# Runs of counts, early projections and 29 dense chunks in a graph layer with a mixture of experts

## The chip, the core and the metric

The kernel runs on one core of one Trainium2 chip. Its engines each work through a queue of their own: TensorE (PE, with PEld for its weight loads), VectorE (DVE), ScalarE (ACT), GpSimd (POOL), and SyncE (SP), which mostly starts DMAs. The metric is the device time of one launch in microseconds (us), the median over several runs.

## The reference

6250 nodes have 256 features each, and 200,000 edges lead from `src` to `dst`, sorted by `dst`. A graph convolution and a residual projection feed a top-2 mixture of 64 experts, then `y` is normalised over the nodes, added to the features, and layer-normed.

```python
deg_out = jnp.clip(jax.ops.segment_sum(ones, src, num_segments=n), 1.0)
deg_in = jnp.clip(jax.ops.segment_sum(ones, dst, num_segments=n), 1.0)
h = feats * jax.lax.rsqrt(deg_out)[:, None]
m = jax.ops.segment_sum(h[src], dst, num_segments=n) * jax.lax.rsqrt(deg_in)[:, None]
gc = m @ W_gc + b_gc
x = gc + (feats @ W_res + b_res)
core = _moe_ff(x, Wg, bg, w1, b1, w2, b2)
y = x + core
```

## The kernel before

**Stages.** The nodes lie in 50 tiles of 125 (`TP`, `NT`), two of which make a pair. The edges lie in groups of 128.

*Degrees.* In 28 turns (`for i in range(NGR // CG)`) DVE builds two tables of matches, `hot_row` and `hot_col`, and PE multiplies them into `degp`, 56 matmuls a turn (L523). Turns 1 to 25 each hold a projection of one pair by `W_res` as well (`residual`, matmuls at L290 in `projected`), whose result ACT copies out of one of the two banks "pr" (L467) and SP writes to `r_dram`. At i = 2 DVE has a long piece of work (`split` of the remaining edges and what follows), and ACT has twelve activations (L507) that wait for its end. Behind the last turn DVE turns `degp` into `degs`, two projections by `W_gc` run (`firsts_p`), `pd` (L557) folds the degrees by tile, and `s_out` is the factor of each node; a chain on DVE then ends in `key`.

*Opening.* For each pair, `halves` takes the projection by `W_gc`, scales it by `s_out` into rows of two parts (ACT the rounded part, L651; DVE the remainder, L653), and SP writes them to `h_dram`. `steps_of` then multiplies the rows by `back` (L666), which leaves each node's difference to its neighbour, and keeps them in SBUF for the dense chunks (`pair_of`, by ACT L669 and DVE L670). Counts of the first chunk run between.

*Dense chunks.* The edges to the low nodes are dense. `_plan` cuts them into chunks (`DENSE`), each with `n` parts of `k` groups, with windows of `w` columns. For each group one matmul, the count (L740), multiplies `lo` (where the source lies in its tile, made by DVE at L709, eight groups at a time) by `hotk` (the window's match, DVE L269, eight at a time). The `k` groups of a part add up in one PSUM bank (pool `ps_c`, five banks). At the end of each part ACT copies the bank into `words` (`put_in`, L723), and DVE adds the part's first column one part later (`carried`, L775). `apart` unpacks `words` into `counts`, and 50 multiplies (L784) of a chunk form the sums of its nodes. The counts for the next chunk but one are put ahead of the multiplies of the running one, part by part at even distances.

*Gather.* The edges to the high nodes are thin: POOL fetches 128 rows of `h_dram` at a time (L615, a ring of eight), and two matmuls add them up (L620, L621), window by window. A window's sums are copied out by ACT (L1071).

*x_step.* While the chunks run, finished pairs of nodes go through the bias, the transposition (L868), the logits (L877) and the top-2, at fixed multiplies of a chunk.

**Order.** The order on each engine is the order of the program text (`tc.manual_schedule()`). `dense()` yields pieces of work with a cost, and a loop behind it puts a gather in whenever the costs added up reach the next multiple of `every`, which spreads the gathers evenly over that sum; behind a window's last gather it holds the next for `HOLD` = 1.5.

What follows the chunks (the rest of the routing, the experts, the normalisations) is not touched by the change.

Of the kernel before, what the change touches and what calls it, by code (L numbers as in the profile page):

```python
# [66 lines left out]
OPENING, SECOND = 48, 80  # L67
# [93 lines left out]
def gnn_moe_kernel(ctx, tc, x_in, x_turned, src, dst, bases, nexts, firsts, parts, lasts, runs, W_gc, b_gc, W_res, b_res, Wg, bg, w1, b1, w2, b2,  # L161
# [76 lines left out]
    with tc.tile_pool(name="edges", bufs=1) as ep, \  # L238
# [37 lines left out]
        pair_of = {p: ep.tile([TP, 2, 2 * D], F32R, name=f"h{p}", tag=f"h{p}") for p in range(KEPT)}  # L276
# [22 lines left out]
        with tc.tile_pool(name="late", bufs=1) as lp, tc.tile_pool(name="both", bufs=2) as bp, \  # L299
# [164 lines left out]
            def residual(t0):  # L464
# [4 lines left out]

            dstf = lp.tile([128, NGR], F32, name="dstf", tag="dst")  # L470
# [14 lines left out]
                    neg[:, ND + c:ND + c + 1]) for c, (g0, k) in enumerate(GATHER)]  # L485
            for i in range(NGR // CG):
# [32 lines left out]
                if i == 10:  # L519
                    placed()  # L520
                for c in range(CG):
                    r = c % 2
                    T.matmul(degp[64 * r:64 * r + NT], hot_col[:, c // 2, :, r],  # L523
                             bytes_of[:, c // 2, :, r, :], start=(c0 + c < 2), stop=(c0 + c >= NGR - 2))
# [30 lines left out]
            firsts_p = [projected(0, banks[1], w_gc), projected(2, spare_bank, w_gc)]  # L555
# [38 lines left out]
        with tc.tile_pool(name="xs", bufs=1) as xs, tc.tile_pool(name="hotg", bufs=2) as hg, \  # L594
# [5 lines left out]
            for i, a, b, clear in ((0, 0, 9, V), (0, 9, NU, G), (1, 0, NU, G)):  # L600
                clear.memset(words[i][:, a:b, :], 0)
# [6 lines left out]
            for i in range(NR):  # L608
# [3 lines left out]
                ring.append(r)  # L612

# [27 lines left out]
            HB = 4  # L641
            after = xs.tile([TP, 2, D + 2], F32, name="z")[:, 0, :TP]
            G.tensor_scalar(after, iota_f[:TP, :TP], -1.0, pidx[:TP], op0=ALU.add, op1=ALU.is_equal)
            back = hg.tile([128, HB, WIN], F32R, name="hot")[:TP, 0, :TP]
            G.tensor_tensor(back, ident[:TP, :TP], after, ALU.subtract)
# [12 lines left out]
            def steps_of(p):  # L658
# [8 lines left out]
                if p >= KEPT:  # L667
                    pair_of[p] = ep.tile([TP, 2, 2 * D], F32R, name=f"h{p}", tag=f"h{p}")
# [28 lines left out]
            lo_bufs = [hc.tile([128, PAIRS // 2, 128, 2], U16, name=f"lo{i}", bufs=1) for i in range(3)]  # L697
            for lo in lo_bufs:
                G.memset(lo[:, :, TP:, :], 0)
                G.memset(lo[:, :, TP:TP + 1, :], UNIT_CODE)  # L700
# [31 lines left out]
            def count(g):  # L732

                c, j, i = groups[g]
                g0, k, w, n = DENSE[c]
                if i == 0:
# [3 lines left out]
                T.matmul(pc, los[g // PAIRS][:, r // 2, :, r % 2, 0], hots[g // PAIRS][:, r // 2, :NU * w, r % 2],  # L740
                         start=(i == 0), stop=(i == k - 1))
                if i == k - 1:
# [4 lines left out]
                    carried(1)  # L747
                    at, pc = live["at"][j % 8], pc.rearrange("p (u w) -> p u w", w=w)
                    if j == 0:
                        live["adds"], live["carry"], live["puts"] = [], [], []  # L750
                    if c == 0 and j == 0:
                        live["puts"].append(put_in(words[0][:, :, :w], pc).ins)
                    else:
                        if j == 0:
                            step = nc.values_load(step_i[0:1, c:c + 1], engines=(DVE_E,), min_val=0, max_val=WIN - 1,
                                                  skip_runtime_bounds_check_because="clipped to the window")
                            put = put_in(words[c % 2][:, :, 1:w], pc[:, :, 1:])
                            to, had = words[c % 2][:, :, 0:1], words[(c - 1) % 2][:, :, ds(step, 1)]
                        else:
                            put = put_in(words[c % 2][:, :, 1:][:, :, ds(at, w - 1)], pc[:, :, 1:])  # L760
                            to = had = words[c % 2][:, :, ds(at, 1)]
                        for a in live["adds"]:
                            tc.declare_no_dep(put.ins, a, reason="other columns of the window")
                        live["carry"].append((to, pc[:, :, 0:1], had, j))
                        live["puts"].append(put.ins)
                if r in making:
                    making[r](g // PAIRS + 2)
                if i == k - 1 and j == n - 1:
                    carried(0)

            def carried(but):

                while len(live["carry"]) > but:
                    to, more, had, j = live["carry"].pop(0)
                    add = V.scalar_tensor_tensor(to, more, 1.0 / UNIT, had, op0=ALU.mult, op1=ALU.add).ins  # L775
                    tc.add_manual_dep(add, live["puts"][j].name, SYNCED, reason="its bank, and the column of the part in front")
                    for a in live["puts"][j + 1:]:
                        tc.declare_no_dep(add, a, reason="columns behind it")
                    live["adds"].append(add)
# [163 lines left out]
            def x_step(c, t):  # L943
# [7 lines left out]
                    ((0, 2, 4, 6), 9, 19, (22, 24, 26, 27), (28, 29, 32, 36, 39))  # L951
# [30 lines left out]
            def dense():  # L982
# [24 lines left out]
                for c in range(1, ND):  # L1007
                    g0, k, w, n = DENSE[c]
                    us = max(0.03 + 0.0071 * w, (n * (0.19 + k * (0.105 + 0.0089 * w)) / 0.85 - 9.0) / (n * k))
                    for j in range(n):  # L1010
                        at = 1 + j * 34 // n if c == 1 else NT * (c - 2) + 35 + j * NT // n
                        todo.setdefault(at, []).extend((us, g) for g in range(g0 + j * k, g0 + j * k + k))
                for c in range(ND):
                    for t in range(NT):
                        for us, g in todo.get(NT * c + t, []):
                            yield us, lambda g=g: count(g)
# [941 lines left out]
```

## Time and profile before

| | us |
|---|---|
| median of 3 runs | 1522.32 |
| lowest and highest run | 1515.85, 1525.04 |
| the profiled execution | 1522.74 |
| its span, first to last instruction | 1521.0 |
| PE busy | 1371.6 (90%) |
| DVE busy | 901.8 (59%) |
| POOL busy | 770.0 (51%) |
| ACT busy | 674.3 (44%) |

In the profile's rows a time stands first, then the engine, the line of the kernel, the operation, what it writes and reads, its shape and how many such instructions follow one another (x56). Brackets show how long the engine was idle before it and what ended that. A matmul's duration is a modelled one and contains the filling of a pipeline, so where matmuls follow one another the distance from start to start says what each takes. In a list of waits, a row names who waited for whom, the us in all, how often, and the longest.

### The profile page before, as it was taken

Reading aid. Unit: us, or ns where it says so; the run is one execution under the profiler, and the core shown is the slowest. Engines: PE = TensorE matmul, PEld = TensorE weight load, DVE = VectorE, ACT = ScalarE, POOL = GpSimd, SP = SyncE. Lnnn points to the kernel's source line nnn. Section 1 sums busy time; section 2 is a strip of 40 time slices with the busy share of each in tenths; the row PEclk is TensorE's granted clock in tenths of the full one; section 3 lists DMA queues with packets and bytes.
Section 4 is the critical chain, followed back from the end, with each engine's and each line's share of the span. In section 5 each row is a group of like instructions: output and inputs, shape, how many; then the busy total and the mean of one; then the engine's idle time right before and its main releaser. Section 6 shows DMA issues by size and latency. Waiting matters only on the chain. (4 is left out here: it accounts for less than half of the span.)

```text
span 1521.0 us, 29996 instructions
## 1 busy us (share of the span) xinstructions
PE 1371.6 (90%) x8943; PEld 1054.2 (69%) x8943; DVE 901.8 (59%) x2514; ACT 674.3 (44%) x1938; POOL 770.0 (51%) x871
## 2 busy tenths in 40 slices
PE   3997988898999999999999984899999999997995
PEld 3786866566767666666666764788798887886652
DVE  9997776575776766666666647523233332221887
ACT  1232554345565666665566632322222233332257
POOL 6201037777776676665566611266566666663000
PEclk8998999899999999999999995899999999999997
DMA  9463748787888889887888737888699898785925
GB/s 282 133 174 101 218 139 219 201 245 232 242 248 239 232 228 250 227 237 206 222 221 242 214 101 160 211 250 270 191 287 280 259 300 248 238 267 165 266 76 149
DMA packets 214161, 329.79 MB, mean 217 GB/s; under 512 B 36844, under 2 KB 149008, under 8 KB 213988
## 3 DMA queue, kind: packets, MB, share of 16 engines
q1 hardware_dynamic: 159392, 173.57, 42.0%
q0 software_dynamic: 47696, 147.12, 32.3%
q10 hardware_dynamic: 6900, 7.07, 1.6%
q8 instruction: 74, 1.21, 0.3%
q14 instruction: 99, 0.81, 0.2%
HBM read 266.53 MB, written 73.68 MB: 224 GB/s over the span
## 5 line engine op out<-in xcount | busy, mean ns | idle before, releaser
L615 POOL DMA_INDIRECT r<-h_dram,srcg x441 | 459.2, 1041 | 286.1 <-PE pc L740 160.4
L784 PE MATMUL sm<-h,counts 125*128 125x512 f32 x1500 | 530.5, 441 | 0.0
L723 ACT ACTIVATE words<-pc 128x119 f32 (+7 forms) x682 | 191.2, 280 | 249.5 <-PE pc L740 230.1
L784 PEld LDWEIGHTS sm<-h,counts 125*128 125x128 f32 x1500 | 258.2, 197 | 10.3 <-issue 1.9
L1656 ACT ACTIVATE hT<-ph,b1c 128x128 f32<-128x128 f32 (+3 forms) x256 | 108.2, 423 | 295.1 <-PE ph L1654 272.8
L775 DVE SCALAR_TENSOR_TENSOR words<-pc,words 128x17 f32 x681 | 125.7, 185 | 139.0 <-ACT words L723 114.7
L1654 PE MATMUL ph<-xgT,w1s 128*128 128x128 f32 (+8 forms) x1024 | 206.6, 348 | 0.9 <-issue 0.9
L740 PE MATMUL pc<-hotk,lo 128*128 128x136 bf16 (+6 forms) x1122 | 198.7, 233 | 4.7 <-DVE words L775 2.7
L729 ACT ACTIVATE counts<-words 125x1152 fp32r<-125x1152 uint8 (+1 forms) x180 | 197.4, 1098 | 0.3 <-DVE words L775 0.3
L1691 PE MATMUL py<-w2s,hT 128*128 128x256 f32 (+1 forms) x800 | 192.7, 384 | 0.0
L1654 PEld LDWEIGHTS ph<-xgT,w1s 128*128 128x128 f32 x1024 | 170.7, 192 | 29.0 <-issue 9.9
L1615 POOL DMA_INDIRECT y_dram<-ys,dest x124 | 119.1, 961 | 114.6 <-DVE ys L1669 59.8
L740 PEld LDWEIGHTS <-lo 128*128 128x128 fp8e5 x1122 | 86.4, 101 | 128.2 <-issue 105.3
L1615 POOL DMA_INDIRECT xg<-x_dram,ids x124 | 120.3, 970 | 86.9 <-DVE ids L1295 47.8
L620 PE MATMUL pg<-r,hot 128*128 128x258 f32 x441 | 139.0, 315 | 22.0 <-DMA r<-h_dram,srcg 20.6
L1691 PEld LDWEIGHTS py<-w2s,hT 128*128 128x128 f32 (+1 forms) x800 | 144.4, 188 | 20.5 <-issue 0.3
L1669 DVE TENSOR_TENSOR ys<-py,b2s 128x256 f32<-128x256 f32 (+3 forms) x124 | 52.4, 423 | 165.8 <-PE py L1691 136.6
L621 PE MATMUL pg<-r,hot 128*128 128x256 f32 x441 | 125.1, 284 | 0.0
L1639 DVE COPY xgT<-pte 128x256 f32<-128x256 f32 (+8 forms) x64 | 38.5, 601 | 131.7 <-PE pte L1637 131.7
L709 DVE TENSOR_TENSOR lo<-place_in,floor_in 128x1000 uint16<-128x1000 uint16 x141 | 95.4, 676 | 30.7 <-PE pc L740 25.3
L620 PEld LDWEIGHTS pg<-r,hot 128*128 128x128 f32 x441 | 85.7, 194 | 37.3 <-DMA r<-h_dram,srcg 22.5
L269 DVE TENSOR_TENSOR hotk<-key,iota 128x1088 bf16<-128x1088 bf16 (+6 forms) x141 | 98.4, 698 | 4.1 <-issue 4.1
(403 smaller groups left out, 1845.7 us busy)
## 6 DMA issues: line engine op xcount, KB each, us to landing
w1s<-in_L_gnn_w_dram SPq DMA_DIRECT2D x64, 512.0 KB
w2s<-in_L_gnn_w_dram SPq DMA_DIRECT2D x64, 512.0 KB
y_dram<-h_dram SPq DMA_DIRECT2D x97, 128.0 KB
yr<-y_dram SPq DMA_DIRECT2D x25, 448.0 KB
b2s<-in_L_gnn_b_dram SPq DMA_DIRECT2D x64, 128.0 KB
r<-h_dram,srcg POOLq DMA_INDIRECT x441
z_dram<-zeros ACTq DMA_DIRECT2D x7, 903.0 KB
x<-in_x_turned_dram SPq DMA_DIRECT2D x12, 500.0 KB
```

What stands on the lines that cost most here:

```text
L615: G.indirect_dma_start(out=f32(r[:, :2 * D]), out_offset=None, in_=h_dram[:, :], in_offset=bass.IndirectOffsetOnAxis(ap=idx, axis=0))
L620: T.matmul(pg, hot, r[:, D:], start=first, stop=False)
L621: T.matmul(pg[:, :D], hot, r[:, :D], start=False, stop=last)
L723: return S.activation(to, pc, AF.Copy, scale=1.0 / UNIT)
L729: S.activation(counts[:, t0:t1, :], each[:TP, u:u + t1 - t0, :WIN, b], AF.Copy, accum_out=read_sums[:, 6 * c + i:6 * c + i + 1])
L740: T.matmul(pc, los[g // PAIRS][:, r // 2, :, r % 2, 0], hots[g // PAIRS][:, r // 2, :NU * w, r % 2], start=(i == 0), stop=(i == k - 1))
L775: add = V.scalar_tensor_tensor(to, more, 1.0 / UNIT, had, op0=ALU.mult, op1=ALU.add).ins
L784: T.matmul(sm, counts[:, t, :], hrow(t), start=(t == 0), stop=(t == NT - 1))
L1615: w = G.indirect_dma_start(**kw)
L1654: T.matmul(ph[:, :m], w1s[:, kk, c * 128:(c + 1) * 128], xgT[:, kk, :m], start=(kk == 0), stop=(kk == 1))
L1656: S.activation(hT[:, c, :m - apart], ph[:, :m - apart], AF.Gelu, bias=b1_e[:, c:c + 1])
L1691: T.matmul(py[:n], hT[:, c, k * 128:k * 128 + n], w2s[:, c, :], start=(c == 0), stop=(c == 3))
```

## The change

- *Runs of eight.* The counts of a chunk are put ahead of a multiply in runs that begin at each eighth group (`PAIRS`, the groups that one `lo` and one `hotk` serve) or at a chunk's first, not part by part. Up to three parts lie side by side in a bank (`most_of`). ACT copies a bank's parts when the last is counted (`copied_in`), and DVE adds their first columns one bank later.
- *Pacing.* The counts and the x_step have no cost of their own in the pacing sum; each multiply carries `step_us(c)`, taken from the chunks whose counts run then.
- *Plan.* `SECOND` is 112 in place of 80. The plan then has 29 dense chunks in place of 30, 1116 dense groups in place of 1122, and 447 gathered groups in 28 windows in place of 441 in 27.
- *Early projections.* `firsts_p` goes. Twelve pairs (`EARLY_P`) are projected by `W_gc` while the degrees are counted: one ahead of turn 0, three after turn 0's counts, seven ahead of turn 2's, one after turn 26's. ACT copies them into `early_p`. `w_gc` is loaded right behind the first part of x, ahead of `w_res`. The kept pairs take other buffers (`new_pair`).
- *The odd ones of the twelve* are scaled by POOL (two instructions a pair), ACT only copies them, and POOL takes the remainder in place of DVE (two more a pair).
- *Clearing in order of use.* POOL clears the ends of `lo` first, makes `back`, scales the first odd pair, clears its part of `words[0]`, scales the other odd pairs, sets the ring, and then clears `words[1]`.
- *x_step.* The turn comes at the 11th step in place of the 9th, the logits at the 20th in place of the 19th, the top-2 from the 23rd in place of the 22nd.

```diff
-OPENING, SECOND = 48, 80
+OPENING, SECOND = 48, 112
...
+        EARLY_P = KEPT
+        early_p = [ep.tile([TP, 2, 2, D], F32, name=f"p{j}", tag=f"h{j}") for j in range(EARLY_P // 2)]
...
             x_quad(0)
+            nc.sync.dma_start(out=w_gc, in_=W_gc.rearrange("(k p) d -> p k d", p=128))
+            x_quad(1)
             nc.sync.dma_start(out=w_res, in_=W_res.rearrange("(k p) d -> p k d", p=128))
-            for q in range(1, QUADS):
+            for q in range(2, QUADS):
                 x_quad(q)
-            nc.sync.dma_start(out=w_gc, in_=W_gc.rearrange("(k p) d -> p k d", p=128))
...
+            def ahead_of_degrees(p):
+                pr = projected(2 * p, ps_a.tile([128, 512], F32, name="pr"), w_gc)
+                S.copy(early_p[p // 2][:, p % 2], pr)
+
+            jobs = {-1: range(0, 1), 0: range(1, 4), 2: range(4, EARLY_P - 1), NGR // CG - 2: range(EARLY_P - 1, EARLY_P)}
...
+            for p in jobs[-1]:
+                ahead_of_degrees(p)
             for i in range(NGR // CG):
...
+                if i == 2:
+                    for p in jobs[2]:
+                        ahead_of_degrees(p)
                 for c in range(CG):
...
                 if 0 < i <= NT // 2:
                     residual(2 * i - 2)
+                if i != 2:
+                    for p in jobs.get(i, ()):
+                        ahead_of_degrees(p)
...
-            firsts_p = [projected(0, banks[1], w_gc), projected(2, spare_bank, w_gc)]
...
-            for i, a, b, clear in ((0, 0, 9, V), (0, 9, NU, G), (1, 0, NU, G)):
-                clear.memset(words[i][:, a:b, :], 0)
+            lo_bufs = [hc.tile([128, PAIRS // 2, 128, 2], U16, name=f"lo{i}", bufs=1) for i in range(3)]
+            for lo in lo_bufs:
+                G.memset(lo[:, :, TP:, :], 0)
+                G.memset(lo[:, :, TP:TP + 1, :], UNIT_CODE)
+            after = xs.tile([TP, 2, D + 2], F32, name="z")[:, 0, :TP]
+            G.tensor_scalar(after, iota_f[:TP, :TP], -1.0, pidx[:TP], op0=ALU.add, op1=ALU.is_equal)
+            HB = 4
+            back = hg.tile([128, HB, WIN], F32R, name="hot")[:TP, 0, :TP]
+            G.tensor_tensor(back, ident[:TP, :TP], after, ALU.subtract)
+            for p in range(1, EARLY_P, 2):
+                for u in range(2):
+                    one = early_p[p // 2][:, 1, u, :]
+                    G.tensor_scalar(one, one, s_out[:, 2 * p + u:2 * p + u + 1], None, op0=ALU.mult)
+                if p == 1:
+                    for clear, a, b in ((V, 0, 9), (G, 9, NU)):
+                        clear.memset(words[0][:, a:b, :], 0)
...
+            G.memset(words[1], 0)
...
             def halves(t):
-                ps = firsts_p[t // 2] if t < 4 else projected(t - 1, (banks[1], spare_bank)[t // 2 % 2], w_gc)
+                p = t // 2
+                ps = early_p[p // 2][:, p % 2] if p < EARLY_P else projected(t - 1, (banks[1], spare_bank)[p % 2], w_gc)
+                scaled = p < EARLY_P and p % 2
                 rows = held_rows[t // 2] = [stages[(u - NT) % len(stages)] for u in (t - 1, t)]
                 for u in range(2):
-                    S.activation(rows[u][:, :D], ps[:, u, :], AF.Copy, scale=s_out[:, t - 1 + u:t + u])
+                    if scaled:
+                        S.copy(rows[u][:, :D], ps[:, u, :])
+                    else:
+                        S.activation(rows[u][:, :D], ps[:, u, :], AF.Copy, scale=s_out[:, t - 1 + u:t + u])
                 for u in range(2):
-                    V.scalar_tensor_tensor(rows[u][:, D:], ps[:, u, :], s_out[:, t - 1 + u:t + u], f32(rows[u][:, :D]),
-                                           op0=ALU.mult, op1=ALU.subtract)
+                    if scaled:
+                        G.tensor_tensor(rows[u][:, D:], ps[:, u, :], f32(rows[u][:, :D]), ALU.subtract)
+                    else:
+                        V.scalar_tensor_tensor(rows[u][:, D:], ps[:, u, :], s_out[:, t - 1 + u:t + u],
+                                               f32(rows[u][:, :D]), op0=ALU.mult, op1=ALU.subtract)
...
                 if i == 0:
-                    live["pc"] = ps_c.tile([128, 512], F32, name="pc")
-                r = g % PAIRS
-                pc = live["pc"][:, :NU * w]
+                    if j == 0:
+                        carried(0)
+                        live["adds"], live["puts"], live["ended"] = [], [], []
+                    most = most_of(c)
+                    if j % most == 0:
+                        live["bank"] = ps_c.tile([128, 512], F32, name="pc")
+                    live["pc"] = live["bank"][:, j % most * NU * w:(j % most + 1) * NU * w]
...
+                    if j % most_of(c) == most_of(c) - 1 or j == n - 1:
+                        copied_in(c)
...
+            def most_of(c):
+                return min(3, 512 // (NU * DENSE[c][2]))
+
+            def copied_in(c):
+                w, bank = DENSE[c][2], []
+                carried(1)
+                for j, at, pc in live["ended"]:
...
-                    ((0, 2, 4, 6), 9, 19, (22, 24, 26, 27), (28, 29, 32, 36, 39))
+                    ((0, 2, 4, 6), 11, 20, (23, 25, 26, 27), (28, 29, 32, 36, 39))
...
-                        todo.setdefault(at, []).extend((us, g) for g in range(g0 + j * k, g0 + j * k + k))
+                        for g in range(g0 + j * k, g0 + j * k + k):
+                            if g % PAIRS == 0 or g == g0:
+                                run = todo.setdefault(at, [])
+                            run.append(g)
+
+                def spent(c):
+                    if c >= ND:
+                        return 13.0, 5.0
+                    g0, k, w, n = DENSE[c]
+                    return 13.9 + n * k * (0.02 + 0.0071 * w), 5.0 + n * (0.19 + k * (0.105 + 0.0089 * w))
+
+                def step_us(c):
+                    te, ve = (0.7 * a + 0.3 * b for a, b in zip(spent(c + 1), spent(c + 2)))
+                    return max(te / 0.83, ve / 0.78) / NT
...
-                        yield 0.22, lambda c=c, t=t: multiply(c, t)
+                        yield step_us(c), lambda c=c, t=t: multiply(c, t)
                         if 4 <= t < 44:
-                            yield 0.04, lambda c=c, t=t: x_step(c, t)
+                            yield 0.0, lambda c=c, t=t: x_step(c, t)
```

More of the change, by code (lines that the diff above doesn't have):

```diff
@@ L275, in gnn_moe_kernel, with new_pair @@
         KEPT = NT // 2 - QUADS
-        pair_of = {p: ep.tile([TP, 2, 2 * D], F32R, name=f"h{p}", tag=f"h{p}") for p in range(KEPT)}
+        EARLY_P = KEPT
+        early_p = [ep.tile([TP, 2, 2, D], F32, name=f"p{j}", tag=f"h{j}") for j in range(EARLY_P // 2)]
+        pair_of = {}
+        def new_pair(p):
+            to = p + EARLY_P // 2 if p < KEPT - EARLY_P // 2 else p - KEPT + EARLY_P // 2 if p < KEPT else p
+            pair_of[p] = ep.tile([TP, 2, 2 * D], F32R, name=f"h{p}", tag=f"h{to}")
+        for p in range(KEPT - EARLY_P // 2):
+            new_pair(p)
         quad_of = [ep.tile([128, 4, 2, TP], F32, name=f"x{q}", tag=f"h{KEPT + q}", padded_shape=[128, 4, 2, 128])
@@ L666, in steps_of @@
                         T.matmul(bank[:, u, :], back, rows[u][:, k * D:(k + 1) * D], start=(k == 0), stop=(k == 1))
-                if p >= KEPT:
-                    pair_of[p] = ep.tile([TP, 2, 2 * D], F32R, name=f"h{p}", tag=f"h{p}")
+                if p not in pair_of:
+                    new_pair(p)
                 S.copy(pair_of[p][:, :, :D], bank)
@@ L746, in count @@
                             skip_runtime_bounds_check_because="clipped to what the window leaves")
[L747 to L750, printed above, removed]
+                    live["ended"].append((j, live["at"][j % 8], live["pc"].rearrange("p (u w) -> p u w", w=w)))
+                    if j % most_of(c) == most_of(c) - 1 or j == n - 1:
+                        copied_in(c)
@@ L751, in count @@
+                if r in making:
+                    making[r](g // PAIRS + 2)
+                if i == k - 1 and j == n - 1 and c in (0, ND - 1):
+                    carried(0)
+            def most_of(c):
[4 more added lines that the diff above has]
+                for j, at, pc in live["ended"]:
                     if c == 0 and j == 0:
                         live["puts"].append(put_in(words[0][:, :, :w], pc).ins)
-                    else:
[L754 to L769, printed above, removed]
+                        continue
+                    if j == 0:
+                        step = nc.values_load(step_i[0:1, c:c + 1], engines=(DVE_E,), min_val=0, max_val=WIN - 1,
+                                              skip_runtime_bounds_check_because="clipped to the window")
+                        put = put_in(words[c % 2][:, :, 1:w], pc[:, :, 1:])
+                        to, had = words[c % 2][:, :, 0:1], words[(c - 1) % 2][:, :, ds(step, 1)]
+                    else:
+                        put = put_in(words[c % 2][:, :, 1:][:, :, ds(at, w - 1)], pc[:, :, 1:])
+                        to = had = words[c % 2][:, :, ds(at, 1)]
@@ L771, in carried @@
+                    for a in live["adds"]:
+                        tc.declare_no_dep(put.ins, a, reason="other columns of the window, another bank")
+                    bank.append((to, pc[:, :, 0:1], had))
+                    live["puts"].append(put.ins)
+                live["carry"].append((bank, len(live["puts"])))
+                live["ended"] = []
             def carried(but):
                 while len(live["carry"]) > but:
-                    to, more, had, j = live["carry"].pop(0)
@@ L775, in carried @@
[L775 to L779, printed above, removed]
+                    bank, upto = live["carry"].pop(0)
+                    for to, more, had in bank:
+                        add = V.scalar_tensor_tensor(to, more, 1.0 / UNIT, had, op0=ALU.mult, op1=ALU.add).ins
+                        tc.add_manual_dep(add, live["puts"][upto - 1].name, SYNCED,
+                                          reason="its bank, and the column of the part in front")
+                        for a in live["puts"][upto:]:
+                            tc.declare_no_dep(add, a, reason="columns behind it, another bank")
+                        live["adds"].append(add)
```

17 lines of the change are left out of this document (4 added, 13 removed).

## The prediction

> **What bounds the kernel now.** I read the page's engine table first, then the busy time by stage, then the chain. The chain that ended last covers only the final pass over the output, so the stages themselves say what the change is worth. They are the degrees (0 to 127.5 us), the opening in which h is written (to 198.5), the first four dense chunks (to 324), the other 26 (to 909), and the experts and the output, which the change does not touch.
>
> ```profile
> span 1521.0 us, 29996 instructions
> 0.00:127.50 127.50, 101.46 (x1770) 84.75 (x1771) 120.92 (x103) 29.65 (x87) 32.56 (x108) 0.93 0.68 191
> 127.50:198.50 71.00, 61.62 (x344) 53.87 (x344) 50.14 (x120) 33.25 (x79) 5.11 (x27) 0.93 0.55 168
> 198.50:324.00 125.50, 105.73 (x706) 75.80 (x706) 80.88 (x220) 54.26 (x157) 86.21 (x79) 0.90 0.72 196
> 324.00:909.00 585.00, 553.94 (x3215) 397.99 (x3213) 385.64 (x1396) 348.09 (x1063) 372.97 (x362) 0.99 0.81 224
> ```
>
> The columns are PE, PEld, DVE, ACT and POOL busy, the granted clock, the DMA share and GB/s. In the last row PE is busy for 554 of 585 us and no other engine for more than 386. So PE sets this stage, and what PE has to do there is what counts. Its time is read from start to start in the timeline of PE.
>
> ```profile
> 256.73 0.42 PE L740 MATMUL pc<-hotk,lo 128*128 128x136 bf16 x4
> 256.96 0.48 PE L784 MATMUL sm<-h,counts 125*128 125x512 f32 x1
> ...
> 503.92 0.39 PE L784 MATMUL sm<-h,counts 125*128 125x512 f32 x1
> 504.16 0.22 PE L740 MATMUL pc<-hotk,lo 128*128 128x102 bf16 x1
> 504.20 0.47 PE L784 MATMUL sm<-h,counts 125*128 125x512 f32 x1
> 504.51 0.22 PE L740 MATMUL pc<-hotk,lo 128*128 128x102 bf16 x1
> ```
>
> A multiply that follows an fp32 matmul takes 0.24 us (503.92 to 504.16). One that follows a count takes 0.31 (504.20 to 504.51), and the count itself 0.04. So every place where a run of counts ends costs 0.04 + 0.08 = 0.12 us, and a count with another behind it costs 0.075 (four counts of 136 columns take 0.23).
>
> **The change part by part.** *Runs of counts, 29 chunks, 447 gathers.* I counted through dense() and the pacing loop by their source, for the old plan and the new. For the old one this gives 742 counts and 366 gathers from the fifth chunk on and 75 gathers before it, which the rows confirm up to one count.
>
> ```profile
> 324.00:909.00 585.00, 154.52 (x743) 63.25 (x741) 0.99 0.81 224
> ...
> 198.50:324.00 125.50, 26.36 (x75) 14.90 (x75) 0.90 0.72 196
> 324.00:909.00 585.00, 112.63 (x366) 70.83 (x366) 0.99 0.81 224
> ```
>
> From the fifth chunk on there are 1300 multiplies, 611 ends of runs and 131 counts with another behind them. After the change there are 1250, 106 and 594, with 366 gathers as before. That is -50 x 0.234 = -11.7, -505 x 0.12 = -60.6 and +463 x 0.075 = +34.7: **-37.6 us**. At these prices (0.24 a gather, 0.65 a window of gathers) the old stage comes to 489 us of its 585. The other 96 us are the x_step work (23 pairs in both versions), waits and halved clock. One chunk of 26 less takes some 3.5 us of that, which makes **-41**.
>
> In the first four chunks the runs save little, because 3 to 11 groups a part are runs already, and the chunks grow: the prices give 98.8 us before and 100.8 after, with 81 gathers for 75. POOL is the tight one here, with fetches end to end:
>
> ```profile
> 244.40 0.95 POOL L615 DMA_INDIRECT r<-h_dram,srcg  x1 [0.30 <-issue]
> 245.65 0.94 POOL L615 DMA_INDIRECT r<-h_dram,srcg  x1 [0.30 <-issue]
> ```
>
> Six more at 1.25 us are +7.5 and PE's own sum is +2.0. I take **+5**, near POOL's end.
>
> The waits of that stage are the unknown. The rows below are for 206 to 910 us.
>
> ```profile
> POOL r L615 <- PE pc L740: 160.4, 173, 69.1
> DVE words L775 <- ACT words L723: 114.7, 160, 4.4
> PE pg L620 <- DMA r<-h_dram,srcg: 20.6, 14, 3.9
> PE sm L868 <- DVE xr L858: 14.3, 17, 1.8
> L723 ACT ACTIVATE words<-pc 128x119 f32 (+7 forms) x682 | 191.2, 280 | 249.5 <-PE pc L740 230.1 <-PE pg L621 3.7 <-PE sm L784 2.7
> ```
>
> The waits of ACT and DVE cost nothing while PE runs. PE's 14.3 us on xr should shrink, since the turn comes two multiplies later and DVE no longer waits for ACT after every part. Against that, eight copies in a row hold ACT for 8 x 0.28 = 2.24 us, and the copy of a finished gather window stands behind them, with PE's next gather behind that copy. Bounds: -10 (the xr waits mostly gone), +12 (28 windows at 0.4). I take 0. Banks are no new wait: a run of eight fills 2.7 of five, and DVE empties them a run later. The new pacing and the later x_step turns add no instruction and are priced in these counts and waits.
>
> *Twelve projections during the degrees.* These rows show PE and ACT in that stage.
>
> ```profile
> 19.28 2.10 PE L523 MATMUL degp<-hot_row,hot_col 128*50 128x128 fp8e4 x56 [2.17 <-DVE hot_col L492]
> 21.31 3.26 PE L290 MATMUL pr<-w_res,x 128*125 128x256 f32 x8
> 30.97 2.16 ACT L507 ACTIVATE wide<-kd 128x44 f16<-128x44 bf16 x12 [13.24 <-DVE first L418]
> 33.03 0.56 ACT L467 COPY rx<-pr 125x512 f32<-125x512 f32 x1
> 36.11 3.19 PE L523 MATMUL degp<-hot_row,hot_col 128*50 128x128 fp8e4 x56 [11.53 <-DVE hot_col L492]
> 42.00 1.75 PE L523 MATMUL degp<-hot_row,hot_col 128*50 128x128 fp8e4 x56
> ...
> 121.42 1.99 PE L290 MATMUL pr<-w_res,x 128*125 128x256 f32 x8
> 123.34 1.75 PE L523 MATMUL degp<-hot_row,hot_col 128*50 128x128 fp8e4 x56
> 125.70 1.75 PE L523 MATMUL degp<-hot_row,hot_col 128*50 128x128 fp8e4 x56 [0.60 <-DVE hot_col L492]
> ```
>
> A projection takes 1.92 us of PE (121.42 to 123.34), so twelve take 23. PE's holes here are 2.17, 11.53 and 0.60 us, with perhaps 2 before the first count: 17 us, and a delay of 6 us at least. It will be more. Seven projections are put ahead of the counts of i = 2, for the hole of 11.53. But "pr" has two banks, so the third needs ACT's copy of the first, and this copy stands on ACT behind the twelve L507, which wait for DVE until 30.97. The rows show it: the residual that began at 21.31 was copied only at 33.03. So two projections run by 28, PE then stands until 33.13 + 0.58 = 33.7, and five follow: 9.6 us, and 1.5 more because PE comes out of a pause slowly (the counts at 36.11 took 3.19 us, those at 42.00 1.75). That is 44.8. The counts and the residual of i = 2 (3.6) and the counts and residual of i = 3 (3.6) put the counts of i = 4 at 52.0 instead of 42.0. From there both run at PE's 3.6 us a turn, the late one without some 2 us of mask waits that the old one has in 42.00 to 123.34 (22 turns, 81.3 us). The twelfth projection adds 1.92 before the last counts, where PE waited 0.60 anyway. Sum: the last counts start at 42 + 10 + 22 x 3.6 + 1.7 + 1.9 = 134.8 instead of 125.7, **+9**; bounds +6 and +11.
>
> What is gained behind it: the two old projections no longer stand in front of pd.
>
> ```profile
> 128.94 0.22 DVE L554 TENSOR_TENSOR degs<-dsb,rise 128x63 f32<-128x63 f32 x1
> 130.94 0.32 PE L557 MATMUL pd<-fold,degs 128*125 128x50 f32 x2
> ```
>
> degs is ready at 129.2, so pd moves by **-1.7**, and s_out with the key chain behind it.
>
> *The opening.* POOL is let go at 136.2 (call it T), and pairs leave PE every 2.36 us.
>
> ```profile
> 136.21 2.89 POOL L601 MEMSET words<- 128x1056 int32 x2 [25.03 <-issue]
> 145.31 1.42 PE L666 MATMUL pc<-r,hot 125*125 125x256 f32 x4
> 150.71 0.83 PE L666 MATMUL pc<-r,hot 125*125 125x256 f32 x4
> 153.07 0.82 PE L666 MATMUL pc<-r,hot 125*125 125x256 f32 x4
> L643 POOL TENSOR_SCALAR z<-iota_f,pidx 125x125 f32<-125x125 f32 x1 | 0.7, 738 | 0.0
> L1745 POOL TENSOR_TENSOR fb<-fb,bet 125x512 f32<-125x512 f32 x1 | 1.3, 1276 | 0.0
> ```
>
> The second pair's steps ran at T + 9.1. Now that pair's low half is POOL's, and in POOL's order it stands behind everything that is cleared and behind all twelve scalings: small clears and "back" 2, scalings 12 x c, clearing 0.9 + 0.6 + 2.0, then two subtractions of 0.7 (half of the 512-wide row). For c the row with two operations on 125 columns gives 0.74, twice that for the width is 1.5; with one operation instead of two I take 0.8. Sum 16.5: the second pair comes at T + 16.8, **+7.7**. Clearing in order of use thus hides nothing here, as the scalings are the longer part. Pairs 3 to 12 then have no projection. An odd one takes ACT 0.4, POOL 1.4, PE 0.7 and ACT 0.6 in a chain that the even one fits beside: 3.4 us for two instead of 4.7, **-6.7** over ten pairs, and 1.5 for PE's slow start: **+2.5**. With c at 0.5 it is -1, with 1.5 it is +11. The remaining pairs go on at 2.36.
>
> Sum: 9 - 1.7 + 2.5 + 5 - 41 = -26. Against this execution (1522.74 us around its span of 1521.0, 0.4 above the median of 1522.32) that is **1497 us**.
>
> **A rule against a row.** The Trainium skill, TensorE: Matmul & The Clock Gate, LDWEIGHTS (loading the stationary operand), gives a weight load the number of its columns over 1.2, 107 ns for the 128 here. By that rule a count behind a count would take 0.107 and the runs would save next to nothing: 919 counts x 0.032 = 29 us dearer, 1526. The four counts at 256.73, spaced at 0.075 or less, speak against it.
>
> **The rivals.** *A, the forecast*, 1497.
> *B, within 1%: bursts.* The bursts on ACT and the denser gathers make PE wait. 28 windows at 0.8 us (a third of a burst) give 22 us: 1519. For it, POOL at its 1.25 us in the first chunks; against it, POOL is busy 373 of 585 us later on. The rule above would end here too.
> *C, slower: POOL starved.* One row speaks for it, 256 columns in 2.51 us while DVE compared without a pause:
>
> ```profile
> L516 POOL TENSOR_TENSOR bsum<-bsum,bres 125x256 f32<-125x256 f32 x1 | 2.5, 2508 | 0.0
> ```
>
> With 2.5 us for each of the 24 operations the second pair comes at T + 40.5 (+31.4), and two pairs take 7 us (+11.4). The opening is +44 instead of +2.5: 1539. It decides from about 2.5 us an operation; at 1.9 the gain is just gone. The Trainium skill, SBUF — State Buffer, Who interferes with whom, says that a Vector instruction with two SBUF inputs and a GpSimd one that reads SBUF exclude each other for the whole instruction. The new even pairs read two SBUF tiles on DVE. Against C: DVE has little to do while the scalings run.
> *D, the change's early part costs nothing:* ACT's order does not bind and c is 0.5: 6 - 1.7 - 1 + 5 - 41 = -33, 1490; it lies in A's range.
>
> **How the numbers follow.** A and D 0.62, B 0.25 and the weight rule 0.04, C 0.09. A's ends are 6 - 1.7 - 1 + 2 - 47 (waits -6) = -42, and 11 - 1.7 + 11 + 7.5 - 29 (waits +12) = -1. The range is 1480 to 1520 and holds B's price. Within 1% (15 us), about what a measurement of this kernel can tell from no change, are B and the weight rule. Faster 0.62, same 0.29, slower 0.09.
>
> **What would show it.** Counts eight in a row at 0.07 to 0.08 us, and 100 to 110 ends of runs from the fifth chunk on; a stage of about 675 us from the first multiply instead of 710. In the degrees a pause of PE until about 33 us, ended by ACT, and last counts near 135. In the opening the second pair's steps held by POOL until some 17 us after POOL starts. I would be wrong if PE waits in the dense stage rise by more than 20 us, or if POOL's scalings take over 1.9 us.

## The result, and the profile after

| | before | changed |
|---|---|---|
| median of the runs, us | 1521.49 (4 runs, 1515.85 to 1525.04) | 1543.49 (4 runs, 1540.89 to 1545.48) |
| ratio | | 1.0147, 95% interval 1.0111 to 1.0183 |
| profiled execution, its span | 1522.74, 1521.0 | 1544.83, 1542.9 |

The change made the kernel 22 us slower; the forecast was 26 us faster. These are the stages of the changed kernel, from the page and from the busy time by stage. The columns are those of the rows before: PE, PEld, DVE, ACT and POOL busy, granted clock, DMA share, GB/s. The last row is that of the counts (L781) alone, with PE, PEld, clock, DMA share and GB/s.

```profile
span 1542.9 us, 29083 instructions
0.00:138.90 138.90, 121.44 (x1865) 100.79 (x1865) 120.64 (x102) 36.16 (x97) 22.94 (x109) 0.98 0.63 176
138.90:213.70 74.80, 50.49 (x250) 41.54 (x248) 46.17 (x108) 33.75 (x81) 26.14 (x51) 0.73 0.52 161
213.70:347.10 133.40, 110.82 (x770) 86.67 (x770) 96.21 (x250) 58.05 (x165) 95.91 (x86) 0.94 0.70 199
347.10:933.00 585.90, 519.41 (x3106) 421.12 (x3104) 390.40 (x1347) 349.97 (x1025) 374.12 (x362) 0.96 0.79 223
...
347.10:933.00 585.90, 64.45 (x700) 44.54 (x700) 0.96 0.79 223
```

| stage | before | changed | difference | forecast |
|---|---|---|---|---|
| degrees | 127.5 | 138.9 | +11.4 | +9 |
| degrees' end to the first multiplication | 71.0 | 74.8 | +3.8 | +0.8 (-1.7 + 2.5) |
| first four chunks | 125.5 | 133.4 | +7.9 | +5 |
| the other chunks | 585.0 | 585.9 | +0.9 | -41 |
| the rest of the span | 612.0 | 609.9 | -2.1 | 0 |

The stages are cut at round times. The first multiplication itself starts at 198.5 and 213.4 us.

The miss lies in the fourth row. PE did become less busy there, 519 us instead of 554, and the counts went from 154.5 to 64.5 us; the stage did not become shorter. So PE stood still instead.

To split this I took the trace's matmuls from the first multiplication to the last. For each triple of kinds (the matmul in front, this one, the one behind) the median time from start to start, at most 0.45 us, is its plain price; what goes beyond the plain prices is the excess, that is waits and halved clock. Before: 637 us plain and 73 in excess. Changed: 593 plain and 126 in excess. The plain work fell by 44 us, and the excess rose by 53. From the fifth chunk on, the stage for which 41 us less was forecast, the plain work fell by 48 (539 to 492) and the excess rose by 49 (45 to 94); the first four chunks have 4 more of each.

Who ended the waits stands in PE's list of waits from 206 to 934 us: total, times, longest.

```profile
PE sm L921 <- DVE xr L911: 25.0, 14, 3.7
PE pg L658 <- DMA r<-h_dram,srcg: 23.7, 22, 2.5
PE pg L658 <- ACT resg L1137: 13.1, 9, 2.8
PE sm L837 <- ACT picked L978: 9.3, 8, 2.3
```

Against before: xr 14.3, the fetches 20.6; for the copy of a gather window and for the copies of the ranks

```profile
PE pg L620 <- ACT resg L1071: 1.2, 3, 0.6
```

and no row for the ranks at all. So xr brought +10.7, the window's copy +11.9 and the ranks' copies +9.3 us; the fetches, which the denser gathers should have hurt, +3.1. All of PE's time without a matmul, from the first multiplication to the last, went from 51 to 89 us. These 38 us and up to 12 of halved clock (last section) make up nearly all of the 53.

The first three stand behind a run. This is the timeline of the changed kernel around one run of eight:

```profile
704.21 0.67 PE L781 MATMUL pc<-hotk,lo 128*128 128x136 bf16 x8
705.24 0.60 PE L1135 MATMUL pg<-resg,overg 128*128 128x258 f32 x2
705.49 1.29 PE L837 MATMUL sm<-h,counts 125*128 125x512 f32 x4
705.53 1.05 ACT L765 ACTIVATE counts<-words 125x1024 fp32r<-125x1024 uint8 x1
706.57 0.19 ACT L904 ACTIVATE s_in<-s_in 125x2 f32<-125x2 f32 x1
706.66 0.89 ACT L759 ACTIVATE words<-pc 128x119 f32 x3
706.79 0.17 DVE L908 RECIPROCAL s_in<-s_in 125x2 f32<-125x2 f32 x1 [4.52 <-ACT s_in L904]
708.34 0.91 ACT L759 ACTIVATE words<-pc 128x119 f32 x3 [0.79 <-ACT words L759]
709.13 0.37 ACT L1137 COPY resg<-pg 128x258 f32<-128x258 f32 x1
709.55 0.39 PE L658 MATMUL pg<-r,hot 128*128 128x258 f32 x1 [2.78 <-ACT resg L1137]
709.98 0.63 DVE L827 SCALAR_TENSOR_TENSOR words<-pc,words 128x17 f32 x3 [0.91 <-DVE words L827]
710.52 0.72 DVE L269 TENSOR_TENSOR hotk<-key,iota 128x1088 bf16<-128x1088 bf16 x1
711.16 0.48 DVE L911 SCALAR_TENSOR_TENSOR xr<-z,s_in,xr 125x256 f32<-125x256 f32 x1
711.69 0.68 PE L921 MATMUL sm<-ident,xr 125*128 125x125 f32 x2 [1.14 <-DVE xr L911]
```

The window of gathers ends on PE at 705.84. Its copy is ACT's work of 0.37 us, but starts at 709.13: ACT goes through its queue in order, and ahead stand the last of the next chunk's L765, which was there before the change too, and six copies of counts, with a pause of 0.79 us between the two banks that was not followed up. PE's next gather waits 2.78 us for it. Then DVE's queue: its additions for the same six parts, and the next "hotk", stand ahead of the second half of xr, and PE waits 1.14 us for that. In the kernel before, the parts came one at a time, each with its copy of 0.28 us.

### The profile page after: what moved, and what is told of

Read it like the earlier page. It is cut to its first block, busy times and chain, and to the rows that moved or that the text cites. A ratio compares the mean times of both kernels' runs of the same rounds, so it can differ in the third digit from the quotient of the medians.

```text
span 1542.9 us, 29083 instructions
## 1 busy us (share of the span) xinstructions
PE 1350.2 (88%) x8900; PEld 1091.5 (71%) x8900; DVE 918.1 (60%) x2483; ACT 686.9 (45%) x1919; POOL 793.7 (51%) x902
## 5 line engine op out<-in xcount | busy, mean ns | idle before, releaser
L653 POOL DMA_INDIRECT r<-h_dram,srcg x447 | 470.0, 1052 | 260.3 <-PE pg L659 124.2
L837 PE MATMUL sm<-h,counts 125*128 125x512 f32 x1450 | 484.0, 428 | 9.9 <-ACT picked L978 9.3
L837 PEld LDWEIGHTS sm<-h,counts 125*128 125x128 f32 x1450 | 253.8, 198 | 32.1 <-ACT picked L978 12.0
L759 ACT ACTIVATE words<-pc 128x136 f32 (+7 forms) x665 | 185.9, 280 | 202.3 <-PE pc L781 163.5
L765 ACT ACTIVATE counts<-words 125x1152 fp32r<-125x1152 uint8 (+1 forms) x174 | 188.4, 1090 | 1.5 <-DVE words L827 0.8
L827 DVE SCALAR_TENSOR_TENSOR words<-pc,words 128x17 f32 (+1 forms) x664 | 124.1, 187 | 61.4 <-ACT words L759 34.2
L659 PE MATMUL pg<-r,hot 128*128 128x256 f32 x447 | 129.3, 289 | 0.0
L781 PE MATMUL pc<-hotk,lo 128*128 128x153 bf16 (+5 forms) x1116 | 103.3, 230 | 7.7 <-ACT words L759 4.1
L269 DVE TENSOR_TENSOR hotk<-key,iota 128x1224 bf16<-128x1224 bf16 (+5 forms) x140 | 99.6, 711 | 9.5 <-issue 9.5
L1114 DVE TENSOR_TENSOR hot<-keyg,iota_f 128x512 fp32r<-128x512 f16 (+3 forms) x121 | 78.0, 646 | 43.7 <-PE pg L659 42.9
```

Of the source, the lines that this page charges most:

```text
L653: G.indirect_dma_start(out=f32(r[:, :2 * D]), out_offset=None, in_=h_dram[:, :], in_offset=bass.IndirectOffsetOnAxis(ap=idx, axis=0))
L659: T.matmul(pg[:, :D], hot, r[:, :D], start=False, stop=last)
L759: return S.activation(to, pc, AF.Copy, scale=1.0 / UNIT)
L765: S.activation(counts[:, t0:t1, :], each[:TP, u:u + t1 - t0, :WIN, b], AF.Copy, accum_out=read_sums[:, 6 * c + i:6 * c + i + 1])
L781: T.matmul(live["pc"], los[g // PAIRS][:, r // 2, :, r % 2, 0], hots[g // PAIRS][:, r // 2, :NU * w, r % 2], start=(i == 0), stop=(i == k ...
L837: T.matmul(sm, counts[:, t, :], hrow(t), start=(t == 0), stop=(t == NT - 1))
```

## The experiments

The table has all kernels. First multiplication, plain and excess are of the profiled execution, in us. Each ratio is to executions of the kernel before that were taken along with it, whose medians lie between 1521.4 and 1522.1.

| kernel | median | ratio to before, 95% interval | first multiplication | plain | excess |
|---|---|---|---|---|---|
| before | | | 198.5 | 637 | 73 |
| changed | 1543.5 | 1.0147 (1.0111 to 1.0183) | 213.4 | 593 | 126 |
| early projections alone | 1538.0 | 1.0101 (1.0066 to 1.0136) | 214.8 | 637 | 74 |
| runs alone | 1526.6 | 1.0020 (0.9999 to 1.0042) | 197.3 | 592 | 128 |
| runs of four | 1523.0 | 1.0012 (0.9989 to 1.0036) | 214.8 | 597 | 98 |
| copies spread | 1508.3 | 0.9906 (0.9873 to 0.9938) | 214.0 | 592 | 90 |
| spread, old front | 1494.6 | 0.9815 (0.9787 to 0.9842) | 198.0 | 591 | 95 |
| spread, mended front | 1490.3 | 0.9798 (0.9772 to 0.9825) | 193.7 | 591 | 89 |
| changed, copies ahead | 1535.0 | 1.0077 (1.0053 to 1.0100) | 202.5 | 593 | 135 |
| changed, scalings between | 1534.2 | 1.0070 (1.0042 to 1.0098) | 205.0 | 593 | 126 |
| runs of sixteen | 1567.2 | 1.0304 (1.0269 to 1.0339) | 213.2 | 584 | 162 |
| spread, mended, 30 chunks | 1518.4 | 0.9985 (0.9964 to 1.0005) | 195.5 | 600 | 111 |
| changed, three copies on VectorE | 1545.1 | 1.0150 (1.0119 to 1.0181) | 213.7 | 596 | 125 |
| spread, mended, three copies on VectorE | 1485.8 | 0.9773 (0.9748 to 0.9799) | 194.1 | 591 | 90 |

**The two halves of the change.** One kernel has the early projections and the clearing alone (every other hunk undone), one has the rest alone.

> The kernel before with the early projections and the clearing in order of use alone: counts part by part, old pacing, 30 chunks. Theory A (the degrees' stage and the opening became about 15 us longer, from the start of the first multiplication in the two traces, 198.5 against 213.7, and the runs lost the rest): the time before plus 11 to 16 us, 1533 to 1538, and the waits of TensorE in the dense stage as before (excess over the usual spacing near 73 us). Rival (the later start is bought back by an opening whose multiplications are no longer held): within 5 us of before.

> The changed kernel with the early projections and the clearing undone: runs of eight, three parts a bank, the new pacing, 29 chunks. Theory A: the dense stage is 9 us longer than before, as in the trace of the changed kernel, and the front as before: 1526 to 1532. Rival (the dense stage lost by starting in another rhythm, behind an opening in which POOL's queue was late): faster than before by 10 us or more, under 1512.

Measured: 1538.0, that is 15.9 us over its runs of before (1522.1), and 1526.6, 4.5 us over, with an interval that just reaches no difference. Together 20.4, and the whole change cost 22: the halves add. The excess of 126 to 128 us goes with the runs, whatever the front does, and the 15 to 16 us of a later start go with the projections. The new pacing and the later x_step turns are in every kernel with runs, so none of these experiments prices them alone.

**Bursts of half the length.**

```
-                            if g % PAIRS == 0 or g == g0:
+                            if g % 4 == 0 or g == g0:
```

> The changed kernel with runs of four groups in place of eight. Theory A (bursts of up to eight copies and more in ScalarE's queue hold the square root, the window's copy and the ranks' copies, for which TensorE then waits): about 100 more ends of runs at 0.08 us add 8 us of TensorE, the waits that grew (some 45 us with the halved clock) shrink by about half: 1520 to 1532. Rival B (the waits come from the pacing or from the early gathers, not from ScalarE's bursts): 1546 to 1556.

Measured: 1523.0. Over the dense stage the ends of runs rose from 153 to 273, the plain work by 4 us, and the excess fell by 28. The pacing and the gathers' places were not changed, so they did not make those 28 us.

**Bursts spread, runs kept.** PE's order stays. From the third chunk to the last but one a finished bank goes to a list, and one bank of up to three parts is copied out at every second multiplication. DVE's additions are issued along with the copies, so they are spread too.

```
                     if j % most_of(c) == most_of(c) - 1 or j == n - 1:
-                        copied_in(c)
+                        live["late"].append((c, live["ended"]))
+                        live["ended"] = []
...
+                        elif t % 2:
+                            yield 0.0, lambda: late_copies(max(0, len(live["late"]) - 1))
                         yield step_us(c), lambda c=c, t=t: multiply(c, t)
```

> The changed kernel with TensorE's runs kept and ScalarE's copies out of the counts' banks spread from the third chunk on: one bank's three parts at every second multiplication behind the run. Theory A (ScalarE's bursts): TensorE's order is the same, and the waits for the square root's followers, for the window's copy and for the ranks' copies fall towards those of before, 20 to 45 us less: 1500 to 1524. Rival B (pacing): within 6 us of the changed kernel, 1537 to 1549. Rival C (a bank is held longer, so counts wait for one): over 1549.

Measured: 1508.3, 35 us below the changed kernel. Its waits of PE from 206 to 898 us:

```profile
PE pg L658 <- DMA r<-h_dram,srcg: 23.9, 25, 3.4
PE sm L929 <- DVE xr L919: 15.6, 13, 3.7
PE pc L783 <- DVE words L835: 9.2, 4, 4.2
...
PE pg L658 <- ACT resg L1149: 2.1, 3, 1.1
PE sm L845 <- ACT picked L986: 1.4, 1, 1.4
```

The waits for xr, for the window's copy and for the ranks went from 25.0, 13.1 and 9.3 to 15.6, 2.1 and 1.4 us, near those of before, and the plain work kept its 592. PE's matmuls from the first multiplication to the last come in the same order in both traces, all 3874. This shows the cause: the runs' saving on PE was real, and the bursts of copies and additions behind each run took it back. How much of that is ACT's burst and how much DVE's this kernel does not tell. Of the 53 us of excess 36 went; in the 17 that stay, the waits for DVE to let go of a bank are up from 2.7 to 9.2 us and those for fetches from 20.6 to 23.9.

**Longer bursts.** The same line with 2 * PAIRS.

> The changed kernel with runs of sixteen groups. Theory A (ScalarE's burst is what TensorE waits for): the plain spacings fall by some 4 us more, the excess over them goes on as from four (97.7 us) to eight (126.0), 15 to 35 us more: 1555 to 1575. Rival (the excess at eight has another cause, and longer runs only save): 1535 to 1543.

Measured: 1567.2, in the expected range, and 162 us of excess, 36 more, at its upper end. But it was not by the waits that I had in mind:

```profile
PE pc L781 <- DVE words L827: 34.4, 25, 3.8
PE sm L837 <- ACT picked L978: 20.6, 13, 3.8
...
PE sm L921 <- DVE xr L911: 12.1, 6, 6.2
PE pc L781 <- DVE hotk L269: 8.6, 3, 6.9
PE pg L658 <- ACT resg L1137: 7.5, 6, 3.6
```

Of the three only the ranks' wait grew. The largest is new: in the chunks where a part is one group, sixteen groups end sixteen parts, which fill six banks where there are five, so PE waits within a run until DVE's additions let go of a bank. At eight groups this row was 3.6 us. So longer runs cost more, but they do not test the three waits.

**The same bursts, three copies elsewhere.** The window's copy and, likewise, the ranks' two copies are issued on VectorE.

```
-                    S.copy(res, live["pg"])
+                    V.tensor_copy(res, live["pg"])
```

> The changed kernel, its runs and its bursts as they are, with the copy of a finished gather window and the two copies of the ranks moved from ScalarE to VectorE. Theory A (these copies stood behind the bursts): TensorE's waits for the window's copy (13.1 us) and for the ranks' copies (9.3 us) go to near nothing, and some of the halved clock with them: 1514 to 1530; the waits for xr stay near 25 us. Rival (VectorE's queue stands behind the same copies, for its additions wait for ScalarE, so these copies come no sooner): 1538 to 1549.

Measured: 1545.1; the rival was right. The ranks' wait went down to 1.3 us, but the window's stayed at 13.6. The timeline of this kernel shows DVE's queue ahead of the copy:

```profile
542.85 0.60 PE L1134 MATMUL pg<-resg,overg 128*128 128x258 f32 x2
542.92 2.63 ACT L759 ACTIVATE words<-pc 128x102 f32 x9
545.49 0.62 DVE L827 SCALAR_TENSOR_TENSOR words<-pc,words 128x17 f32 x3
546.02 0.65 DVE L269 TENSOR_TENSOR hotk<-key,iota 128x952 bf16<-128x952 bf16 x1
546.59 0.62 DVE L827 SCALAR_TENSOR_TENSOR words<-pc,words 128x17 f32 x3
547.12 0.48 DVE L911 SCALAR_TENSOR_TENSOR xr<-z,s_in,xr 125x256 f32<-125x256 f32 x1
547.51 0.42 DVE L1136 COPY resg<-pg 128x258 f32<-128x258 f32 x1
547.99 0.58 PE L658 MATMUL pg<-r,hot 128*128 128x258 f32 x1 [3.61 <-DVE resg L1136]
```

Each run leaves a burst on both engines, nine copies of 2.63 us on ACT here and the additions behind them on DVE, so moving what stands behind it from one queue to the other does not help. The burst has to be broken up. The Trainium skill, TensorE: Matmul & The Clock Gate, section "Architectural detail: the array is 16× 32×32, not 1× 128×128", calls the queues of ACT and DVE strictly first in, first out; both timelines agree.

**The degrees.** One mend of the changed kernel: the loop over jobs[2] stands ahead of the loop that issues ACT's twelve small scalings (eleven with 29 chunks).

```
+                    for p in jobs[2]:
+                        ahead_of_degrees(p)
                     for g, h, w in wides:
                         S.activation(wide[:, g:h], past_1[:, g:h], AF.Copy, scale=0.5 * w)
```

> The changed kernel with one mend: ScalarE's copies of the seven projections ahead of its twelve small scalings. Theory (TensorE stands 7.57 us behind those scalings): the counts of the third step start near 37 in place of 45.07, the last ones near 129 in place of 137.18, the time 1533 to 1538. Rival (VectorE's chain sets that end, so the stretch is filled anyway): 1541 to 1546.

In the changed kernel two projections ran, and the next came when ACT had done those scalings:

```profile
32.07 2.06 ACT L525 ACTIVATE wide<-kd 128x44 f16<-128x44 bf16 x11 [7.83 <-DVE first L428]
34.03 1.04 ACT L482 COPY p<-pr 125x512 f32<-125x512 f32 x2
34.65 10.49 PE L299 MATMUL pr<-picked,x 128*125 128x256 f32 x40 [7.57 <-ACT p L482]
45.07 1.75 PE L544 MATMUL degp<-hot_row,hot_col 128*50 128x128 fp8e4 x56
...
137.18 1.75 PE L544 MATMUL degp<-hot_row,hot_col 128*50 128x128 fp8e4 x56
```

With the copies ahead the seven run without a pause, and the counts come 9.8 us earlier, both the third step's and the last:

```profile
23.08 12.25 PE L299 MATMUL pr<-picked,x 128*125 128x256 f32 x56
35.26 1.75 PE L543 MATMUL degp<-hot_row,hot_col 128*50 128x128 fp8e4 x56
...
127.38 1.75 PE L543 MATMUL degp<-hot_row,hot_col 128*50 128x128 fp8e4 x56
```

The median is 1535.0, 8.5 us less. (The profiled execution, 1544.3, was the slowest of its ten, with a longer dense stage; the rows of its front are not touched by that.)

**The opening.** The other mend: POOL scales the next odd pair behind the subtraction of the one in front, and clears words[1] at the end.

```
+                if scaled and p + 2 < EARLY_P:
+                    scale_early(p + 2)
+                elif scaled:
+                    G.memset(words[1], 0)
```

> The changed kernel with one mend: POOL's scaling of each odd pair between the subtractions, the second window's clearing behind the last of them. Theory (ten scalings, 9.42 us, and the clearing, 1.97 us, stand ahead of the first subtraction, on which the second pair's differences wait): the second pair's steps start near 155 in place of 166.3, the first multiplication near 203 to 206 in place of 213.7, the time 1531 to 1537. Rival (ScalarE and VectorE set the opening's end, POOL's lateness is made up): within 4 us of the changed kernel.

The changed kernel's POOL began at 146.05, and PE stood until it had scaled everything:

```profile
152.51 9.42 POOL L635 TENSOR_SCALAR p<-p,s_out 125x256 f32<-125x256 f32 x10
162.33 1.97 POOL L650 MEMSET words<- 128x2244 int32 x1
164.30 1.40 POOL L691 TENSOR_TENSOR r<-p,r 125x256 fp32r<-125x256 f32 x2
...
165.07 1.26 PE L706 MATMUL pc<-r,hot 125*125 125x256 f32 x3 [13.29 <-POOL r L691]
```

With the scalings between the subtractions that wait is 2 us, the steps of the second pair come at 154.56, the first multiplication at 205.0, and the median is 1534.2, 9.3 us less:

```profile
154.56 0.79 PE L710 MATMUL pc<-r,hot 125*125 125x256 f32 x2 [2.06 <-POOL r L691]
```

**Together.** The spread copies with the old front, and with both mends.

> Spread copies (the kernel with copies spread, 1508) with the early projections and the clearing undone. If the front and the dense stage simply add, as 1538.0 (early alone) and 1526.6 (runs alone) did: 1508 less 16, 1490 to 1495, first multiplication near 198. Rival (part of the spread's gain hung on the later start, when more of the fetches had landed): over 1500.

> Spread copies with both mends of the front: ScalarE's copies of the seven projections issued ahead of its twelve small scalings, and POOL's scaling of each odd pair issued behind the subtraction of the odd pair in front. Theory: 8 us of the degrees' stage and about 10 us of the opening come back, the first multiplication starts near 196 in place of 214, 1486 to 1496. Rival (the early projections cost TensorE's time wherever they stand, for the degrees' stage is TensorE's): the front keeps most of its 15 us, over 1500.

Measured: 1494.6 and 1490.3. Both are faster than before by more than 1%. Their intervals overlap, so that the mended early projections are worth something is shown only by the traces (first multiplication at 193.7 against 198.0), not by the times.

**What is left.** Two variants of the last kernel: the old plan of 30 chunks (SECOND = 80), and the three copies on VectorE.

> The kernel with copies spread and both mends of the front (1490), with 30 chunks and 441 gathers in place of 29 and 447. The forecast's terms: 50 multiplications more at 0.234 are 11.7 us, some 3.5 us of other work of a chunk, less 2.1 us for six gathers and one window, less up to 7.5 us for POOL's six fetches: 1496 to 1503. Rival (six gathers more hold the stage as long as a chunk does, for fetches are what TensorE waits for most): 1487 to 1494.

> The kernel with copies spread and both mends of the front, and the same three copies on VectorE. With the bursts spread, 2.6 us of TensorE's waits for the window's copy are left: 1485 to 1491. Rival (VectorE's additions and the gathers' comparisons come later by as much): 1491 to 1500.

Thirty chunks give 1518.4, outside both ranges: 28 us dearer. Of this the plain work is some 9, where the forecast's prices for 50 multiplications (11.7) less six gathers and a window (2.1) give 9.6. The excess is 21 us larger, and most of it is at the counts, which wait for DVE's additions to free a bank: 26.7 us in eight waits, where the kernel with 29 chunks has 8.5 in three:

```profile
PE pc L786 <- DVE words L838: 26.7, 8, 5.0
```

Why this plan meets more of them with the copies spread was not followed up, and 30 against 29 chunks was not tried with unspread copies. The three copies on VectorE give 1485.8, the fastest time here; the interval overlaps that of 1490.3.

## Why the prediction was wrong, point by point

- *Runs, plain work:* right. From the fifth chunk on the trace has 106 ends of runs and 594 counts with another behind them, the forecast's numbers to the unit. A count followed by a count took 0.067 us (median) for the forecast's 0.075. The plain work fell by 48 us from the fifth chunk on, for the 41 that the forecast counted on.
- *The waits of the dense stage:* the step that failed. "I take 0", between -10 and +12; it was +49 from the fifth chunk on (+53 with the first four), and the forecast's own bound for being wrong, 20 us more of PE's waits, was passed. The upper bound had one follower of the burst, the copy of a gather window, at 0.4 us each, and for that its total was right: +11.9 over 28 windows. That is partly luck, for the bound took 0.4 us each, and nine of them waited, 1.5 us on average. It left out the others in the same queue, the square root ahead of xr (+10.7, where the forecast had these waits shrink, since the turn comes two multiplications later) and the ranks' copies (+9.3), as well as DVE's burst, and the halved clock that such pauses bring (last section). Spread copies brought the excess from 126 to 90.
- *Rival B (bursts)* had the mechanism, at 22 us and 1519, and a chance of 0.25. Its denser gathers were a small part: waits for fetches grew by 3.1 us.
- *Degrees, +9:* right in mechanism, 11.4. The counts of the third step were expected at 44.8 and came at 45.07; the last at 134.8 and came at 137.18. The 2 us of waits which the later order was to be without did not go away: the turns that took 4.86, 4.05 and 3.98 us before took 4.86, 4.05 and 3.97. Half of that is a wait for `away`, 0.99 us before and 0.98 after, and not for a mask.
- *pd, -1.7:* right: 3.5 us behind the last counts' start (140.69) instead of 5.2.
- *Opening, +2.5:* the order was right, POOL's sum too small. The second pair came at T + 19.0 for the forecast T + 16.8: twelve scalings took 11.4 us for 9.6, and POOL's work ahead of them 3.6 for 2; PE began behind the first of the two subtractions, 0.7 earlier than reckoned. The forecast's own terms add up to 16.5, and the other 0.3 has no term. The opening cost 5.5.
- *First four chunks, +5:* 7.9.
- *One chunk less, 3.5 of other work:* in the kernel with 30 chunks the plain work agrees with the prices (9.2 for 9.6); the rest could not be told apart from the waits for banks.
- *The weight rule* of the rivals did not hold: the counts behind a count took 0.067 us. *POOL starved* did not come: 0.95 us a scaling, 0.70 a subtraction.

The sum without the failed step is 9 - 1.7 + 2.5 + 5 - 41 = -26; with the measured +49 in place of 0 it is +23, against the measured +22. That it comes so close is partly luck: degrees, opening and first four chunks cost 8 us more than forecast, and the plain work of the others (48 for 41) and the rest of the span (-2.1) give 9 back.

## What to carry over

Work that is batched on the engine that bounds the stage comes out as a burst on the engines behind it, and their queues run in order: look at every small instruction that stands behind that burst and on which the bounding engine waits, on all engines that take part, and not only at the busy shares. Batch the one side and spread the other: runs kept on TensorE, with their copies handed out a bank at a time, gave what the runs alone did not. When work is put into an engine's idle time, look at the order in which the helping engines get to it: each of the two early steps lost 8 to 10 us because one loop stood in the wrong place.

## What the runs showed of the hardware

TensorE's clock follows its idle share in a window, and idleness of about half a window is enough to halve it. The granted clock in the traces changes in steps of 3.41 us. In the dense stages of seven of these kernels (before, changed, runs of four and of sixteen, copies spread, spread with the mended front, three copies on VectorE) I took each such window at full clock, and the time in it without a matmul. After 71 windows with 1.9 us or more the next window was at half clock, 71 times; after 1235 with less than 1.6 us, 2 times; in between 13 of 22. In all fourteen kernels of the table the counts are 147 of 147, 2 of 2443 and 35 of 50. So the wait of 2.78 us at 709.55 above is dearer than it looks: the clock was halved from 710.3 to 717.2. Over the dense stage the changed kernel had 65 us at half clock (0.96 in the row of its later chunks, where before had 0.99), the one before 41, the one with spread copies 44. Half of the 24 us more than before, 12 of the 53 us, is the most that this can have cost. The Trainium skill, TensorE: Matmul & The Clock Gate, section "What's actually happening", gives a window of the same 3.4 us and says that the clock drops after at least one idle one. The window agrees with these traces; the condition here is about half an idle window.

POOL's operation on 125 columns that builds "after" took 1.71 us in the changed kernel and 0.74 before, the same instruction at another place. While it ran, DVE worked at "lo" and "hotk" without a pause (147.32 to 149.31), which read two SBUF tensors each; where it took 0.74, DVE ran L653, one of whose two tensors lies in PSUM. Whether the one slows the other no run tests.

```profile
147.10 1.71 POOL L628 TENSOR_SCALAR z<-iota_f,pidx 125x125 f32<-125x125 f32 x1 [0.34 <-issue]
```
